# Handing out the closings of the cross-attention layer at a higher pace, and moving the rows' additions

## The chip, the cores and the metric

The kernel runs on one core of a Trainium2 chip. The metric is the device time of one execution in microseconds, as the median of several runs. The core has engines with in-order queues of their own: PE (TensorE, the matrix unit; PEld is its loading of weights), DVE (VectorE), ACT (ScalarE), POOL (GpSimd) and SP (SyncE, which here only issues transfers). An instruction waits on semaphores for what it needs, and everything behind it on its engine waits with it.

## The reference, cut to what matters

The model is four layers of cross-attention over 16 batches of 56 tokens (width 256), with a context of 1500 rows of width 128 per batch.

```python
x = _L0_xattn_ref(x, ctx, ...)         # memory attention and a gate
x = _L1_xattn_ref(x, ctx, mask, ...)   # 16 heads, context masked; then layernorm and a GELU feed-forward
x = _L2_xattn_ref(x, ctx, types, ...)  # third layer, below
x = _L3_xattn_ref(x, ctx, mask, ...)   # as L1 with other weights: the fourth layer

def _L2_xattn_ref(...):
    vm = expert_mask(token_type_ids)[..., None]
    mixed = jnp.where(vm, rms_norm(x) @ v_qkv, rms_norm(x) @ l_qkv)   # self-attention, rotary, causal
    x = x + jnp.where(vm, ctx @ v_dense, ctx @ l_dense)
    x = x + softmax(cq @ ck.T) @ cv @ cdense_w                        # 16 heads of 8 over 1500 rows
    mi = rms_norm(x, ln_post_attn_w)
    v_out = jax.nn.silu(mi @ v_gate) * (mi @ v_up) @ v_down
    l_out = jax.nn.silu(mi @ l_gate) * (mi @ l_up) @ l_down
    return x + jnp.where(vm, v_out, l_out)                            # the third layer's closing
```

## The kernel before, in words

Tokens go in four groups (0 to 3) of four batches each. Work items are (layer, group), 16 in all, item k = 4 * layer + group; the third layer is items 8 to 11, the fourth items 12 to 15. Each item has an opening (norm, projections), an attention, and a closing (output projection or feed-forward). While the attention of an item is emitted, a Python generator, the side work, gives out the closing of earlier items and the opening of the next one in pieces between the attention's own instructions. All of this only sets the order in which instructions are emitted and so their place in each engine's queue; on the chip the queues run as the semaphores let them.

**Third layer** (`att2`). Each batch b has six steps, j = 0 to 5. I number them 6 * b + j, from 0 to 95. `weights_pair` is the head of a step: four ones-times-shift products and sixteen key products into four PSUM banks (L1441, L1450), four exponentials on ACT (L1455), and additions of the weights into `all` (L1467), on POOL for all batches but the last, four per step (two in a step with j = 0). Beside it a step has `largest` (scores of batch b + 1 and after: L1404 into four banks, four maxima on DVE, L1409), `sums_chunk` (weights times values of the step before, L1482), and one of `values` (L1387) and `keys` (L1375). Step j = 4 makes the next batch's shift (`shifts`: L1417 to L1420 on DVE, L1424 on PE, the copy L1430 on DVE). Step j = 0 closes the previous batch's sums: a copy on ACT, a product with a mask on POOL (L1493), and a reduction on DVE (L1496). Step j = 1 has `own_sums` (L1508 on PE, which needs the batch's finished `all`; L1514, L1516 on DVE). From step 88 on no `largest` is left.

Two calls of `pace` in a step give out side work: the first after the step's head with the rate from `SHARES[group][behind]` (L1354), the second at its end. Each piece yields its cost in microseconds; a bare `yield` ends the call. If the first call made anything, `largest` is emitted ahead of `sums_chunk`, otherwise after it.

The third layer's closing, `post2`, runs for two groups at a time on rows sorted by token type: three rounds (one expert's rows, rows of both, the other's), each with transposes (L310), six gate and up products (L1642) and four pieces of down products (L1661). Its result goes to `made_rows` in DRAM. `fetch` gathers a group's rows back with two indirect transfers that POOL issues (L1679), and `take` adds them to x on DVE (L1689) and begins the fourth layer's norm: statistics on DVE (L339 to L344), a power on POOL (L320), and the normalised rows xn on POOL (L354). PE then transposes xn (L310), and the query projection follows (L907). `late()` holds the closing of groups 0 and 1 (between items 10 and 12), `fetch(0)`, `take(0)`, `fetch(1)`, `take(1)`, and the closing of groups 2 and 3, which goes into the fourth layer. `take`'s addition is tied to follow the instruction whose name is in `line["drained"]`: in the third layer the last maximum that `largest` emitted.

**Fourth layer** (`rows`). A batch is a unit, u00 to u15: seven score products S (L624), each with a masked minimum on DVE (L627) and an exponential on ACT (L631), and in the middle, after the third S, the weighted sum of the batch two units back, 48 products as built (L642, below AV), whose results DVE and ACT copy out (`rows_out`, L1020, L302). `rows_close` (L979) ends a pair of batches. Side work is stepped after each S. `beside(13)` holds `fetch(2)`, `fetch(3)`, `take(2)`, `take(3)`, then the opening of group 2; the closing of group 0 (`follows`: output projection L1092, norm, L1120, GELU L1127, L1092) came after that opening.

PSUM tiles of matmul results come from one ring of seven banks (`ps_s`): a new tile takes the bank of the seventh tile before it, and waits until that one has been read. The weights tile `pw` comes from a ring of three.

Of the kernel before, what the change touches and what calls it, by code (L numbers as in the profile page):

```python
# [62 lines left out]
def tile_kernel(ctx: ExitStack, tc: tile.TileContext, a, layers=4, groups=NG):  # L63
# [3 lines left out]
    nc = tc.nc  # L67
# [24 lines left out]
    def turn():  # L92
        return psum(ps_s, "sc")
# [4 lines left out]
    def few(w):  # L98
        return small.tile([128, w], F32, tag="few", bufs=8, name="few", padded_shape=[128, 16])
# [222 lines left out]
    def behind(made, name, reason):  # L322

        if name:
            tc.add_manual_dep(
                made.ins, name,
                mybir.DependencyInfo(
                    mybir.DependencyClass.NoSync, mybir.DependencyReason.DATA
                ),
                reason=reason,  # L330
            )
# [196 lines left out]
    def pace(share, kept, most):  # L528

        line["due"] += share  # L530
        made = False
        for _ in range(most):
            if line["due"] <= kept:
                break
            work = next(line["side"], line)
            if work is line:
                line["due"] = 0.0
            elif work:
                line["due"] -= work
                made = True  # L540
            else:
                line["due"] = min(line["due"], 3.0)
                break
        return made

    line, memory_w, halves_of, queries, heads_w, cross, held, begun = {}, [], {}, {}, {}, {}, {}, {}
# [804 lines left out]

    QH = 4 * N
    PAIRS = NC // 2
    SHARES = (2.1, 1.65), (2.1, 1.1), (2.1, 1.7), (1.9, 1.9)  # L1354

    def spread_queries(b):

# [55 lines left out]
    def shifts(b):  # L1413

        made = cross[b]
        nm = few(8)[: 2 * N]
        nc.vector.tensor_reduce(nm, made["mx"], AX.X, ALU.max, negate=True)  # L1417
        both = minus[b % 2]
        nc.vector.tensor_copy(both[:, :, 0].bitcast(F32R), nm)
        nc.vector.tensor_tensor(both[:, :, 1], nm, both[:, :, 0], ALU.subtract)  # L1420
        t = turn()
        for n in range(8):
            half, g = divmod(n, 4)
            nc.tensor.matmul(  # L1424
                t[g * BW : (g + 1) * BW, half * 2 * N : (half + 1) * 2 * N],
                both[:, n, :], ident[: 2 * N, : 2 * N], start=True, stop=True,
                skip_group_check=True,
            )
        shift = small.tile([128, QH], F32R, tag="shift", bufs=2, name="shift")
        nc.vector.tensor_copy(shift, t[:, :QH])  # L1430
        made["shift"] = shift

    def weights_pair(b, j):
# [119 lines left out]
    def att2(gi, state, then, ends):  # L1553

        for k in range(G):
            b = gi * G + k
            for j in range(PAIRS):
# [6 lines left out]
                weights_pair(b, j)  # L1564
                full = pace(SHARES[gi][line["behind"]], -0.8, 1)
                last, n = (b, 2 * j - 2) if j else (b - 1, NC - 2)
# [120 lines left out]
    def take(gi, y):  # L1687
        xf = xs[gi].rearrange("p i d -> p (i d)")
        behind(nc.vector.tensor_add(xf, xf, y), line["drained"], "banks go first")  # L1689
        if gi < 3:  # L1690
            begin_layernorm("L3_ln_q_g", gi)

    def program():
# [15 lines left out]
        def before(k):  # L1709
            if k + 1 < len(items):  # L1710
                states[k + 1] = yield from items[k + 1][0](items[k + 1][4])
# [7 lines left out]
        def beside(k):  # L1719

            yield from line.pop("rest", ())
            if k == len(items) and short:
                while line["closed"] < k:
                    yield
                yield from ending(k - 1, 1)
                return
            if k and k + 1 in (groups, groups + 1):
                begin_layernorm("L1_ln_q_g", k + 1 - groups)
            ahead = before(k)
            if k + 1 < groups:  # L1730
                yield next(ahead)
            if k == groups + 1:
                for rows, zeros in zip(sorted_rows, minus):
                    nc.sync.dma_start(
                        rows.rearrange("(p r) d -> p r d", p=TP),
                        zeros.rearrange("p n m -> p (n m)").unsqueeze(1).to_broadcast([TP, 6, D]),
                    )
            third = 2 * groups - 1 <= k <= 3 * groups
            if k:
                _, _, _, post, gi = items[k - 1]  # L1740
                follows = line["late"] if third else post(gi, states.get(k - 1))
            if k + 1 == 3 * groups:
                while line["stage"] < 3:
                    yield next(follows)
            if k == 3 * groups:
                yield next(follows)
            if k == 3 * groups + 1:
                while line["stage"] < 5:
                    yield next(line["late"], 0)
                yield  # L1750
                yield
                back = fetch(2), fetch(3)
                for _ in range(7):
                    yield
                take(2, back[0])
                yield
                take(3, back[1])
                yield
            if k > groups:
                for work in ahead:  # L1760
                    if isinstance(work, tuple):
                        line["beside"] = 1
                        while line["closed"] < k:
                            yield
                        for _ in range(work[1]):
                            yield next(follows, 0)
                    else:
                        yield work
            line["behind"] = 1
            if third:  # L1770
                if k + 1 == 2 * groups:
                    begin_norm("L2_ln_in_w", 1)
                while not line["end"] or line["stage"] < (0, 1, 2, 2, 4, 4)[k + 1 - 2 * groups]:
                    yield next(follows, 0)
                return
            if k:
                while line["closed"] < k:
                    yield
                yield from follows
                states.pop(k - 1)  # L1780
                if k > len(items) - groups:
                    nc.sync.dma_start(
                        a["out"][gi * T : (gi + 1) * T, :].rearrange("(i p) d -> p i d", p=TP), xs[gi]
                    )
            if k <= groups:
                yield from ahead
            if groups <= k < len(items) - 2:
                layer, group = divmod(k + 2, groups)
                if layer == 2:
                    begin_norm("L2_ln_in_w", group)  # L1790
                else:
                    begin_layernorm(f"L{layer}_ln_q_g", group)
            if k + 1 == len(items) and short:
                while line["pair"] != ("L3", groups - 1, 0):
                    yield
                yield from ending(k, 0)

        def late():

            third = 2 * groups  # L1800

            def at(k):
                return line["k"] > k or line["k"] == k and (line["behind"] or line["beside"])

            for gi in (groups - 2, groups - 1):
                while line["closed"] < groups + gi + 1:
                    yield
                yield from post13(
                    "L1", gi, states[groups + gi],
                    pause=lambda: not at(third if gi == groups - 2 else third + 1),  # L1810
                )
                begin_norm("L2_ln_in_w", gi)
                line["stage"] += 1
            while line["closed"] < third + 2 or not at(third + 2):
                yield
            yield from post2(0)
            yield
            yield
            y = fetch(0)
            for _ in range(4):  # L1820
                yield
            take(0, y)
            line["stage"] += 1
            y = fetch(1)
            for _ in range(4):
                yield
            take(1, y)
            line["stage"] += 1
            while line["closed"] < 3 * groups:
                yield  # L1830
            yield from post2(1)
            line["stage"] += 1

        def ending(k, i):

            _, _, _, post, gi = items[k]
            yield from post(gi, states[k], range(i, i + 1))
            at = gi * T + i * TP
            nc.sync.dma_start(a["out"][at : at + TP, :], xs[gi][:, i])
# [34 lines left out]
    t = turn()  # L1874
# [164 lines left out]
```

## Time and profile before

| | us |
|---|---|
| median of 3 runs (1436.54, 1442.94, 1444.49) | 1442.94 |
| the profiled execution's own time | 1437.15 |
| its span in the trace | 1435.3 |
| PE busy | 1357.3 (95%) |
| third layer: step 0 starts / step 82 / step 85 / step 88 / step 92 | 450.1 / 997.5 / 1016.7 / 1028.8 / 1056.2 |
| fourth layer: first S / u06 starts / u07 starts | 1069.5 / 1187.7 / 1214.7 |
| PE idle from 900 to 1070 / from 1070 to the end | 9.0 / 15.1 |

Starts of steps and units are read from the trace's instructions in order of time: a step starts with its first L1441, a unit with its first L624. In the listings below a timeline line reads: start, length (of merged instructions together), engine, line, operation, output<-input, count, and in brackets the idle time of the engine before it and what ended it. A line of the windows view reads: stretch, its length, then busy time of PE, PEld, DVE, ACT and POOL with counts, the granted PE clock (1.00 is full), DMA share and GB/s.

### The profile page before, as it was taken

The numbers are of one execution on the slowest core, as the hardware profiler recorded it, in microseconds if no ns is written. First come the engines' busy times: TensorE is split into PE (matmuls) and PEld (weight loads), VectorE is DVE, ScalarE is ACT, GpSimd is POOL, SyncE is SP. The second block draws the span as 40 slices with busy tenths as digits, with TensorE's granted clock in tenths as the row PEclk, the third lists the DMA queues.
The fourth block names the chain that finished last, engine by engine and source line by source line (L and its number), as shares of the span: only waits on it lengthen the run. The fifth ranks groups of instructions, "written<-read, shape, count | busy, mean of one in ns | idle before, by whom it ended". The sixth has DMA issues, their size and how long they took to land.

```text
span 1435.3 us, 32417 instructions
## 1 busy us (share of the span) xinstructions
PE 1357.3 (95%) x13638; PEld 938.2 (65%) x13638; DVE 777.7 (54%) x1794; ACT 744.8 (52%) x1703; POOL 526.2 (37%) x567
## 2 busy tenths in 40 slices
PE   6989999999899999999999999999899998999998
PEld 4667677775656556655555556656467776877776
DVE  4444754647575754467545755455565445455641
ACT  2334866756543547445554544444356565557661
POOL 0011001010101677767767768788743112100000
PEclk9999999999999999999999999999999999999998
DMA  7853224232322021110201022131122343333320
GB/s 270 351 191 126 85 89 145 90 112 65 103 76 81 23 82 52 54 56 24 81 31 43 29 71 68 52 103 56 39 82 94 134 152 101 124 118 123 108 89 10
DMA packets 38808, 135.78 MB, mean 95 GB/s; under 512 B 8605, under 2 KB 18493, under 8 KB 34557
## 3 DMA queue, kind: packets, MB, share of 16 engines
q1 hardware_dynamic: 33901, 119.03, 24.1%
q0 software_dynamic: 2592, 10.85, 2.2%
q10 hardware_dynamic: 2160, 3.74, 0.8%
q8 instruction: 109, 1.79, 0.5%
q14 instruction: 46, 0.38, 0.1%
HBM read 129.01 MB, written 4.59 MB: 93 GB/s over the span
## 4 chain that ended last, share of the span: by engine, by line
PE 75%; DVE 12%; ACT 6%; POOL 3%; DMA 3%; issue 1%; SPq 0%; DVEq 0%; POOLq 0%; ACTq 0%
PE sc L642 9%; PE sc L624 8%; PE sc L1092 7%; PE sc L1404 7%; PE sc L1450 4%; PE o L1482 4%; PE sc L1642 4%; DVE mx L1409 3%; PE sc L907 3%; PE sc L1120 3%; PE sc L1387 3%; PE sc L1441 3%; PE sc L1661 2%; PE sc L1375 2%; POOL all L1467 2%; ACT p L302 2%
## 5 line engine op out<-in xcount | busy, mean ns | idle before, releaser
L1467 POOL TENSOR_TENSOR all<-all,pw 125x448 f32<-125x448 f32 x300 | 341.1, 1149 | 125.8 <-ACT pw L1455 114.7
L1409 DVE TENSOR_REDUCE mx<-sc 112x1 f32<-112x500 f32 x384 | 233.4, 669 | 140.6 <-PE sc L1404 140.5
L1455 ACT ACTIVATE pw<-sc 125x448 f32<-125x448 f32 x384 | 177.7, 550 | 102.8 <-PE sc L1450 100.1
L631 ACT ACTIVATE p<-p,few 128x384 f32<-128x384 f32 x224 | 136.9, 611 | 99.3 <-DVE few L627 98.9
L624 PE MATMUL sc<-ktl,qa 128*128 128x384 f32 x448 | 176.9, 504 | 0.0
L627 DVE CUSTOM_DVE_ANT_0 p<-sc,mkl 128x384 f32<-128x384 f32 x224 | 121.8, 551 | 92.1 <-PE sc L624 87.4
L642 PE MATMUL sc<-p,kvl 32*128 32x224 f32 x2160 | 149.5, 353 | 4.7 <-DVE qa L940 3.3
L642 PEld LDWEIGHTS sc<-p,kvl 32*128 32x128 f32 x2160 | 136.3, 185 | 20.5 <-issue 9.6
L642 PE MATMUL o<-p,kvl 32*128 32x224 f32 x720 | 144.6, 352 | 0.0
L143 POOL TENSOR_SCALAR mkl<-m32l 128x384 bf16<-128x384 uint8 x32 | 16.3, 510 | 314.1 <-DVE few L627 292.5
L642 PEld LDWEIGHTS o<-p,kvl 32*128 32x128 f32 x720 | 130.7, 185 | 0.0
L302 ACT ACTIVATE p<-p,few 128x384 f32<-128x384 f32 x224 | 121.1, 608 | 8.6 <-DVE few L618 7.2
L1404 PE MATMUL sc<-ck,qs 32*112 32x500 f32 x768 | 122.5, 626 | 2.8 <-ACT ck L302 1.4
L661 DVE STREAM_TRANSPOSE p<-p 128x768 f32<-128x768 f32 (+1 forms) x96 | 102.8, 1095 | 28.6 <-ACT p L302 28.4
L624 PEld LDWEIGHTS sc<-ktl,qa 128*128 128x128 f32 x448 | 78.8, 190 | 37.4 <-issue 9.0
L1450 PE MATMUL sc<-qs,ck 32*125 32x224 f32 x1536 | 98.8, 355 | 0.0
L320 POOL TENSOR_TENSOR stat<-stat,half_less 112x2 f32<-112x2 f32 (+1 forms) x33 | 23.1, 700 | 201.8 <-DVE stat L344 162.0
L302 ACT ACTIVATE ot<-sc 128x224 f32<-128x224 f32 x64 | 32.0, 609 | 121.1 <-PE o L642 83.5
L1482 PE MATMUL o<-pw,vc 125*32 125x224 f32 x1536 | 93.0, 359 | 0.0
L1482 PEld LDWEIGHTS o<-pw,vc 125*32 125x32 f32 x1536 | 40.2, 109 | 69.9 <-issue 57.2
L1450 PEld LDWEIGHTS sc<-qs,ck 32*125 32x125 f32 x1536 | 77.4, 183 | 1.1
L302 ACT ACTIVATE vc<-sc 125x512 f32<-125x512 f32 x48 | 28.6, 596 | 82.0 <-PE sc L1387 79.2
(286 smaller groups left out, 2360.7 us busy)
## 6 DMA issues: line engine op xcount, KB each, us to landing
kvl<-in_ctx_last SPq DMA_DIRECT2D x30, 768.0 KB, 4.2
kt<-in_ctxT SPq DMA_DIRECT2D x23, 750.0 KB, 5.0
w<-in_L_W SPq DMA_DIRECT2D x16, 1024.0 KB, 4.8
w<-in_L_Wq SPq DMA_DIRECT2D x8, 1024.0 KB, 5.0
w<-in_L_Wo SPq DMA_DIRECT2D x8, 1024.0 KB, 5.6
ktl<-in_ctxT SPq DMA_DIRECT2D x32, 192.0 KB, 2.5
w<-in_L_v_qkv SPq DMA_DIRECT2D x4, 768.0 KB, 6.8
w<-in_L_l_qkv SPq DMA_DIRECT2D x4, 768.0 KB, 4.1
```

Source lines behind the costliest of these rows:

```text
L302: nc.scalar.activation(out, in_, AF.Copy, scale=scale)
L624: line["scored"] = nc.tensor.matmul(sc[:, :LW], u["q"][:, i * 128 : (i + 1) * 128], u["kt"], start=True, stop=True).ins.name
L627: line["drained"] = nc.vector.tensor_tensor_reduce(u["p"][:, i], sc[:, :LW], u["mask"], 1.0, -LOWEST, ALU.add, ALU.min, mn[:, i : i + 1],) ...
L631: nc.scalar.activation(u["p"][:, i], u["p"][:, i], AF.Exp, bias=mn[:, i : i + 1], scale=-1.0, accum_out=den[:, i : i + 1],)
L642: product = nc.tensor.matmul(o[g][:, : RB * BW], y["kv"][part, j, :], y["p"][part, :, j * BW : (j + 1) * BW], start=j == 0, stop=j == LB - ...
L661: nc.vector.transpose(blocks, blocks)
L1404: nc.tensor.matmul(banks[g][: 2 * N, :SW], made["q"][part, rows], made["k"][part, cols], start=True, stop=True,)
L1409: line["drained"] = nc.vector.tensor_reduce(made["mx"][:, half * 4 + g, s : s + 1], banks[g][: 2 * N, :SW], AX.X, ALU.max).ins.name
L1450: nc.tensor.matmul(banks[g][:CP, c * QH : (c + 1) * QH], made["k"][part, at : at + CP], made["q"][part], start=False, stop=c == 1, skip_gr ...
L1455: line["weighed"] = nc.scalar.activation(p[:, :, g * QH : (g + 1) * QH], banks[g][:CP, : 2 * QH].rearrange("p (c n) -> p c n", c=2), AF.Ex ...
L1467: added = engine.tensor_tensor(made["all"][:, cols], made["all"][:, cols] if j else p[:, 0, cols], p[:, c, cols], ALU.add,)
L1482: nc.tensor.matmul(made["o"][part, :QH], made["v"][:, n, part], p[:, r * QH : (r + 1) * QH], start=n == 0, stop=n + 1 == NC, skip_group_ch ...
```

## The change

In the third layer the pace of groups 2 and 3 goes up (1.7 to 2.0 and 1.9 to 2.15). `shifts` now puts its copy's name into `line["drained"]`, so that an addition in `take` stands behind a shift copy if that was emitted last. `late()` gives five bare yields instead of four between `fetch(0)` and `take(0)`. In the fourth layer, `beside(13)` waits until item 12 has closed, and gives out five pieces of the closing of group 0 between fetch and addition, and one more after each addition.

```diff
-    SHARES = (2.1, 1.65), (2.1, 1.1), (2.1, 1.7), (1.9, 1.9)
+    SHARES = (2.1, 1.65), (2.1, 1.1), (2.1, 2.0), (2.15, 2.15)
@@ shifts
-        nc.vector.tensor_copy(shift, t[:, :QH])
+        line["drained"] = nc.vector.tensor_copy(shift, t[:, :QH]).ins.name
@@ beside
             if k == 3 * groups + 1:
                 while line["stage"] < 5:
                     yield next(line["late"], 0)
-                yield
-                yield
+                for _ in range(4):
+                    yield
                 back = fetch(2), fetch(3)
-                for _ in range(7):
+                while line["closed"] < k:
                     yield
+                for _ in range(5):
+                    yield next(follows, 0)
                 take(2, back[0])
-                yield
+                yield next(follows, 0)
                 take(3, back[1])
-                yield
+                yield next(follows, 0)
@@ late, after fetch(0)
-            for _ in range(4):
+            for _ in range(5):
                 yield
```

What this does to the built order of instructions in the program that runs: up to step 64 the two builds are equal. Pieces of closing and opening that stand in each of the last steps (PE order; "before/after largest" tells whether L1482 stands behind or ahead of L1404):

| step | before | after |
|---|---|---|
| 65, 66 | one L1661 piece each | two L1661 pieces each |
| 82 | L1661 piece, before | none, after |
| 83 | two L1661 pieces, before | none, after |
| 84 (batch 14, j = 0) | L1661 piece, before | none, after |
| 85 | none | none |
| 86 | none | L310 of xn of group 0, then two L907 pieces |
| 87 | none | two L907 pieces |
| 88 | L310 of xn of group 0 | none |
| 89 | three L907 pieces | none |
| 90 | one L907 piece | none |

On POOL, `fetch(0)` stood after step 86's additions and now stands between step 83's and step 84's; `fetch(1)` stood after step 88's and now stands after step 85's, directly ahead of the power and xn of group 0; xn of group 1 stood among step 89's additions and now stands ahead of them. On DVE, `take(0)` stood between step 87's maxima and the shift of batch 15 and now stands behind step 85's maxima; `take(1)` now stands behind batch 15's shift copy. In step 84, L1496 now stands ahead of that step's four maxima; before, it stood behind them.

In the fourth layer, with S, AV, T (L310), Q (L907), dn (L1092) and up (L1120), counts in instructions as built, units 6 and 7 read on PE:

```
before  u06: S S S AV48 S S S T1 S T3 Q16 qa16
        u07: S dn8 S dn8 S AV48 S T4 S up1 S up7 up4 wv16 up4 dn16
after   u06: S dn4 S dn8 S dn4 AV48 S S T4 S T1 S T3 Q16 up4 qa16
        u07: S up8 S up4 dn4 S dn2 AV2 dn2 AV46 S dn4 S dn4 S S wv16
```

All other units are equal. ACT gets two more loads of a function table in units 6 and 7 (36 instead of 34 in the program that runs). On SP the loads of the closing's weights (Wo, W1, W2 of group 0) now stand ahead of Wq of group 2.

## The prediction

> **What bounds the kernel now.** I read the page first: PE is busy 95% of the span, so only PE's idle time and its clock can move the total; the change moves products but adds none. Then the two stretches that it touches: PE's timeline with its idle times, POOL's beside it, then DVE's, and last the windows view for the clock.
>
> The page's costliest groups: four L1467 additions a step are 4.6 us of POOL, four maxima 2.4 us of DVE.
>
> ```profile
> L1467 POOL TENSOR_TENSOR all<-all,pw 125x448 f32<-125x448 f32 x300 | 341.1, 1149 | 125.8 <-ACT pw L1455 114.7
> L1409 DVE TENSOR_REDUCE mx<-sc 112x1 f32<-112x500 f32 x384 | 233.4, 669 | 140.6 <-PE sc L1404 140.5
> ```
>
> PE at the end of the third layer: in steps 60 to 87 it idles 0.1 us, then 6.3 us in step 88, for the shift (late behind `take(0)` on DVE) and for xn.
>
> ```profile
> 1030.15 0.47 PE L1441 MATMUL sc<-shift,ones_r 2*125 2x448 f32 x1 [0.42 <-DVE mx L1409]
> 1035.20 0.97 PE L1424 MATMUL sc<-ident,minus 112*32 112x112 f32 x16 [2.93 <-DVE minus L1420]
> 1038.37 0.45 PE L310 MATMUL sc<-ident,xn 112*128 112x112 f32 x1 [2.19 <-POOL xn L354]
> 1039.58 0.82 PE L310 MATMUL sc<-ident,xn 112*128 112x112 f32 x3 [0.76 <-POOL xn L354]
> ```
>
> POOL there, almost without a break; xn stands behind step 87's additions:
>
> ```profile
> 1019.11 4.66 POOL L1467 TENSOR_TENSOR all<-all,pw 125x448 f32<-125x448 f32 x4 [2.35 <-ACT pw L1455]
> 1023.93 4.65 POOL L1467 TENSOR_TENSOR all<-all,pw 125x448 f32<-125x448 f32 x4 [0.16 <-ACT pw L1455]
> 1028.73 1.01 POOL L1679 DMA_INDIRECT back<-made,place  x1
> ...
> 1036.25 0.73 POOL L320 TENSOR_TENSOR stat<-stat,half_less 112x2 f32<-112x2 f32 x1
> 1037.09 2.43 POOL L354 TENSOR_SCALAR xn<-x,stat 112x256 f32<-112x256 f32 x2
> ```
>
> DVE in step 48, where L1496 stands ahead of the maxima as it will in step 84: it waits for POOL, and the maxima start 2.8 us after their products.
>
> ```profile
> 775.85 0.54 DVE L1496 TENSOR_REDUCE rest<-rest 128x56 f32<-128x224 f32 x1 [3.04 <-POOL rest L1493]
> 776.31 2.42 DVE L1409 TENSOR_REDUCE mx<-sc 112x1 f32<-112x500 f32 x4
> ```
>
> The fourth layer's one large wait, in u06:
>
> ```profile
> 1196.11 0.68 DVE L1689 TENSOR_TENSOR x<-x,back 112x512 f32<-112x512 f32 x1
> 1199.23 0.16 DVE L344 TENSOR_SCALAR stat<-stat 112x2 f32<-112x2 f32 x1
> 1201.61 0.34 PE L310 MATMUL sc<-ident,xn 112*128 112x112 f32 x1 [4.86 <-POOL xn L354]
> ```
>
> After both waits the granted clock is halved:
>
> ```profile
> 1034.60:1044.70 10.10, 6.55 (x46) 4.76 (x47) 2.89 (x9) 1.85 (x4) 9.47 (x10) 0.50 0.01 2
> 1201.80:1208.50 6.70, 6.10 (x17) 4.63 (x17) 2.97 (x6) 2.34 (x5) 1.48 (x2) 0.50 0.22 39
> ```
>
> At half the clock the busy time holds half the work: 3.3 and 3.05 us lost.
>
> **The third layer.** Pieces given out sooner (steps 65 to 81) cost nothing: PE has no idle time there to fill or add, and a longer step gives POOL and DVE more room. The result's copy and write leave ACT a step's work before step 82, 12 us ahead of the gather, and wait for nobody.
>
> From step 82 I set t = 0 at its start. Before, steps 82 to 84 took 6.00 + 7.35 + 5.82 = 19.2 us with four L1661 pieces; the same without them are steps 46, 47 and 86: 5.03 + 4.52 + 4.54 = 14.1. So the pieces are worth 5.1 us, and t = 0 is at 997.5 + 5.1 = 1002.6.
>
> A step's first exponential comes 1.3 us after its head, its additions 2.4 us after (1016.67 to 1019.11). Additions of 82: 2.4 to 7.05; of 83 (head at 5.0): 7.4 to 12.1. Then `fetch(0)`, 2.3 us (1028.73 to 1031.01): 14.5. Then step 84's two additions (2.2) and L1493 (0.56): 17.3. Only now can L1496 run, and behind it step 84's maxima. Step 85's head, due at 14.1, needs in the ring of seven the banks of two of step 84's score tiles for its third and fourth tile: 17.3 + 0.5 + two maxima of 0.6 = 19.0. **Wait A**, 4.5 us; no piece covers it, as the L1241 pieces did in step 48.
>
> Step 85's exponentials then start at 20.2, its additions end at 25.9, `fetch(1)` at 28.3. `take(0)` runs behind step 85's maxima at 24.7 (rows long landed); addition 1.15, statistics and its neighbours L1514 and L1516 about 3: 28.8. Power 0.75, xn 2.43: the first half at 30.8, the second at 32.0. PE reaches the transposes at 25.3. **Wait B**: 5.5 + 0.8 = 6.3 us, where step 88's 6.3 and 0.2 in step 91 go away. The shift of 15 is late no more: L1417 to L1420 are done before L1424 in step 88.
>
> Step 87 starts at 39, 88 at 46 (heads 1.4; L1482 0.9; L1404 1.0; L1387 1.1; four L907 pieces of 1.65). Step 88's additions end at 52.9; power and xn of group 1, now ahead of step 89's additions, at 56; those at 60.7. L1508 of step 91 needs them and PE is there at 55.8, since steps 89 and 90 have lost their L907 pieces. **Wait C**: 4.9 us. POOL is the engine that is late next all through.
>
> Clock: after A and B 6.8 us each at half, about 6 busy, as after 1201.8. A's loss delays POOL's input too and is taken partly out of B (net 1.8), B's counts (3.0), C's falls where DVE sets the pace (0.5); before 3.3. Net +2.0. After C, L1496 of batch 14 does not stand behind xn: -0.9 (1055.56 to 1056.75 before).
>
> Sum: 4.5 + 6.3 + 4.9 - 6.5 + 2.0 - 0.9 = **+10.3 us**. Bounds: A at least 0 (banks free in time, as in step 86) and at most 4.5 with the whole 3.05 of its clock; C at least 0 with no clock loss (POOL level with PE, as in steps 60 to 81) and at most 6.5, with additions at the 5.13 us that four took beside DVE at 1031.01. So 10.3 - 6.3 - 5.4 = -1.4 to 10.3 + 1.2 + 1.6 = +13.1; I take the chain's value, as each of its links is a row of the same stage.
>
> **The fourth layer.** dn16 moves from u07 to u06, ahead of AV; its weights are issued where Wq and Wo were (1166.7, 1167.4), 20 us early. Wq waits for Wo's buffer until dn16 ends, AV covers it (Q16 is over 12 us later, the page's 1 MB of Wq lands in 5.0). It is passed on SP by no load that PE needs in u06. On POOL the four issues stay in place. But `take(2)` still stands behind AV's copies on DVE: AV's end to xn was 1194.6 to 1201.6, 7.0 us, and stays so. PE has three S (2.05 us) and now T4 (0.5) in it: the wait goes from 4.86 to 4.4, its clock loss stays. Against it, dn now follows up more closely, with table loads between: 0.78 and 1.16 us in front of L1092 in u11 and u15; AV2 covers most. The two table loads (1.283 us by their row) run on ACT, 15.6 of 27 us busy in u06: nothing. Sum 0; bounds -7.9 (wait and clock loss gone) and +2 (both L1092 waits).
>
> In "ScalarE: Activation LUTs" of the Trainium skill, "What ACT_TABLE_LOAD costs", a switch is a load of about 1283 ns and a drain of about 1380. The row of before has no drain: load at 1233.14, GELU at 1234.44. By the page ACT would lose 5.3 us instead of 2.6, and PE still nothing. "TensorE: Matmul & The Clock Gate", "Why this matters for your kernels", warns of idle gaps over about 3 us; here the clock fell after 2.93 and 2.19 us with work between. By the page waits A and B would each halve the clock, which speaks against the change as the rows do; without any such loss the sum would be 2.0 us less.
>
> **Rivals.**
> - *Only waits B and C* (step 84's DVE order does not hold up PE, for instance since POOL runs ahead): A and its net clock loss go, 10.3 - 6.3 = +4: 1447. Against it: the 3.04 us row of step 48.
> - *Landing was the brake* (ends faster): additions waited for their rows (DVE's timeline has 0.91 and 6.91 us of waiting for back, at 1032.76 and 1048.28). With more steps between, xn would be ready at both transposes: 6.3 + 3.3 and 4.86 + 3.05 us go, 1425. It decides from 7.2 us on, so if xn comes within 2 us of PE at both places. Against it: the rows had landed in u06 too, and POOL and AV set the time there.
> - *No change beyond the order* (A and C both stay away, B takes the place of the old 6.3 us with its clock): 10.3 - 6.3 - 5.4 = -1.4, 1442. For it: POOL kept up in every step before 85.
> - *Slower still*: the third layer's upper bound and both L1092 waits, 13.1 + 2 = +15: 1458.
>
> **How the numbers follow.** The profiled execution took 1437.15, 5.8 us below the median of 1442.94; +10.3 + 0 on the median gives 1453 (1447 to 1457 for this case alone). Chances: forecast 0.58, slower still 0.12, only B and C 0.12, no change 0.10, landing 0.08. 0.5% is 7.2 us, about what a measurement of this kernel tells from no change. Slower: 0.70; same: 0.22; faster: 0.08. The range, without 0.08 below and 0.07 above, is 1440 to 1460.
>
> **What would show it.** After: L1496 of step 84 waiting some 4 us on POOL and step 85's third L1441 on DVE; L310 in step 86 waiting over 4 us on POOL; L1508 of step 91 on POOL; two or three stretches at 0.50; in u06 still 4 us before L310. Wrong if step 85's head comes at once, or if u06's L310 does not wait.

## The result, and the profile after

| | before | after |
|---|---|---|
| median of 9 runs each, us | 1440.61 (1434.03 to 1444.49) | 1450.06 (1443.85 to 1455.03) |
| ratio, with its 95% interval | | 1.0071 (1.0050 to 1.0092) |
| profiled execution, own time / span | 1437.15 / 1435.3 | 1449.21 / 1447.4 |
| step 60 to step 82 | 141.2 | 147.6 |
| step 82 to the fourth layer's first S | 72.0 | 77.3 |
| the two together | 213.3 | 224.9 |
| u06 and u07 | 59.1 | 58.6 |
| first S of u08 to first S of u15 / from there to the end | 119.5 / 69.0 | 119.8 / 69.3 |

The change makes the kernel slower by 0.7%, some 10 us. The forecast was 1453 on a median of 1442.94, a ratio of 1.007. The third layer lost 11.6 us; in the fourth, u06 and u07 won half a microsecond, and the units behind them lost 0.6. All of this is read from step 60 on: the profiled execution of after reaches that step 0.57 us later than that of before, which is no part of the change.

One caution for every stage that is compared with before: its profiled execution was a lucky one. Its own time, 1437.15 us, is 3.5 us below the median of 1440.61, and its mean granted clock was 0.986; of the 75 executions of before that ran beside the experiments, two had 0.986 or more, and their mean was 0.982. After's profiled execution is 0.9 us below its median. So the profile flatters before, by 3.5 to 5.2 us against its medians here.

The page of the kernel after first: span, busy time, and the granted clock in 40 slices.

```profile
span 1447.4 us, 32415 instructions
PE 1364.0 (94%) x13638; PEld 940.5 (65%) x13638; DVE 775.6 (54%) x1794; ACT 749.1 (52%) x1705; POOL 525.5 (36%) x567
...
PEclk9999999999999999999999999999889999999998
```

PE is busy 6.7 us longer for the same 13638 products (1357.3 before), and the clock row has two slices of 8 where the third layer ends: time lost at half clock counts as busy. The idle part is on PE's timeline. Between 1010 and 1075 us these are the five longest pauses, with the wait in brackets:

```profile
1022.73 1.31 PE L1441 MATMUL sc<-shift,ones_r 2*125 2x448 f32 x2 [4.08 <-DVE mx L1409]
1036.04 0.36 PE L310 MATMUL sc<-ident,xn 112*128 112x112 f32 x1 [3.76 <-POOL xn L354]
1037.25 0.82 PE L310 MATMUL sc<-ident,xn 112*128 112x112 f32 x3 [0.85 <-POOL xn L354]
1066.21 0.40 PE L1508 MATMUL sc<-all,l2w 125*32 125x56 f32 x4 [4.37 <-POOL all L1467]
1068.51 0.96 PE L1508 MATMUL sc<-all,l2w 125*32 125x56 f32 x28 [1.89 <-POOL all L1467]
```

They are waits A (step 85), B (step 86, in two halves of xn) and C (step 91, in two halves of `all`), at the places forecast. The old 6.3 us of step 88 are gone. DVE's timeline shows A's cause: the reduction L1496 holds up the four maxima behind it while it waits for POOL's L1493.

```profile
1021.55 0.53 DVE L1496 TENSOR_REDUCE rest<-rest 128x56 f32<-128x224 f32 x1 [6.41 <-POOL rest L1493]
1022.00 2.42 DVE L1409 TENSOR_REDUCE mx<-sc 112x1 f32<-112x500 f32 x4
```

POOL's timeline, from `fetch(0)` to xn of group 0:

```profile
1016.51 1.01 POOL L1679 DMA_INDIRECT back<-made,place  x1 [0.16 <-issue]
1017.83 0.94 POOL L1679 DMA_INDIRECT back<-made,place  x1 [0.30 <-issue]
1018.79 2.22 POOL L1467 TENSOR_TENSOR all<-pw 125x448 f32<-125x448 f32 x2
1020.96 0.56 POOL L1493 TENSOR_TENSOR rest<-rest,tables 128x224 f32<-128x224 f32 x1
1026.41 4.64 POOL L1467 TENSOR_TENSOR all<-all,pw 125x448 f32<-125x448 f32 x4 [4.88 <-ACT pw L1455]
1031.19 0.96 POOL L1679 DMA_INDIRECT back<-made,place  x1
...
1034.76 2.43 POOL L354 TENSOR_SCALAR xn<-x,stat 112x256 f32<-112x256 f32 x2
```

Read it downwards: the two issues of the fetch delay step 84's additions and L1493; PE then waits (A) and brings no new weights, so POOL itself is idle for 4.88 us, until step 85's exponentials; then step 85's additions and `fetch(1)` stand ahead of xn (B). Since POOL idles in the middle of its own backlog, its total (525.5 us) says nothing of the loss.

The windows view in the stretches behind the waits; the granted clock is the third value from the right.

```profile
1022.50:1029.40 6.90, 6.67 (x58) 3.19 (x62) 2.17 (x5) 1.86 (x4) 2.92 (x3) 0.51 0.00 0
1036.20:1043.00 6.80, 5.95 (x34) 2.93 (x34) 2.23 (x5) 0.00 (x0) 5.44 (x5) 0.50 0.01 2
1063.50:1073.70 10.20, 5.59 (x72) 3.52 (x74) 4.16 (x9) 1.86 (x4) 5.32 (x6) 0.50 0.00 0
1220.50:1227.30 6.80, 6.15 (x18) 4.62 (x17) 3.25 (x9) 2.56 (x6) 4.53 (x5) 0.50 0.15 36
```

Behind A and B 6.83 us at half clock each, behind C 10.24, and in u06 the 6.83 that were there before. That wait in u06 is still on the timeline: the addition stands behind AV's copies on DVE, and the normalised rows xn and their transposes follow from it.

```profile
1215.00 0.69 DVE L1689 TENSOR_TENSOR x<-x,back 112x512 f32<-112x512 f32 x1
...
1218.93 2.44 POOL L354 TENSOR_SCALAR xn<-x,stat 112x256 f32<-112x256 f32 x2
...
1220.22 0.32 PE L310 MATMUL sc<-ident,xn 112*128 112x112 f32 x1 [4.05 <-POOL xn L354]
```

### The profile page after: what moved, and what is told of

It reads as the page before. It is cut to its first block, busy times and chain, and to the rows that moved or that the text cites. A ratio compares the mean times of both kernels' runs of the same rounds, so it can differ in the third digit from the quotient of the medians.

```text
span 1447.4 us, 32415 instructions
## 1 busy us (share of the span) xinstructions
PE 1364.0 (94%) x13638; PEld 940.5 (65%) x13638; DVE 775.6 (54%) x1794; ACT 749.1 (52%) x1705; POOL 525.5 (36%) x567
## 5 line engine op out<-in xcount | busy, mean ns | idle before, releaser
L1404 PE MATMUL sc<-ck,qs 32*112 32x500 f32 x768 | 124.2, 631 | 2.8 <-ACT ck L302 1.4
L1482 PE MATMUL o<-pw,vc 125*32 125x224 f32 x1536 | 95.1, 366 | 0.2 <-ACT rest L302 0.2
L1482 PEld LDWEIGHTS o<-pw,vc 125*32 125x32 f32 x1536 | 40.8, 110 | 69.7 <-issue 56.8
```

What stands on the lines that cost most here:

```text
L1404: nc.tensor.matmul(banks[g][: 2 * N, :SW], made["q"][part, rows], made["k"][part, cols], start=True, stop=True,)
L1482: nc.tensor.matmul(made["o"][part, :QH], made["v"][:, n, part], p[:, r * QH : (r + 1) * QH], start=n == 0, stop=n + 1 == NC, skip_group_ch ...
```

## The experiments

Twelve kernels were run, each against the kernel before. "Third" is the stretch from step 60 to the fourth layer's first S in the profiled execution, in us; its part from step 82 on is called the tail (72.0 us in before, 77.3 in after). The stage carries a doubt of its own: run e2 has the third layer of before unchanged and measured 216.2 instead of 213.3, from one stretch at half clock that is told of at the end.

| run | kernel | ratio to before | 95% interval | third | u06+u07 |
|---|---|---|---|---|---|
| | before | 1 | | 213.3 | 59.1 |
| | after | 1.0071 | 1.0050 to 1.0092 | 224.9 | 58.6 |
| e1 | before + pace | 1.0007 | 0.9988 to 1.0026 | 219.2 | 59.4 |
| e2 | before + fourth layer's part | 0.9994 | 0.9973 to 1.0015 | 216.2 | 58.7 |
| e3 | after, maxima first | 1.0010 | 0.9990 to 1.0030 | 220.1 | 58.6 |
| e4 | after, three pieces | 1.0028 | 0.9999 to 1.0057 | 224.2 | 53.9 |
| e5 | after, four bare yields | 1.0013 | 0.9999 to 1.0027 | 217.3 | 58.4 |
| e6 | after, additions on DVE | 1.0082 | 1.0061 to 1.0103 | 222.4 | 59.5 |
| e7 | before + tie and fifth yield | 1.0001 | 0.9988 to 1.0014 | 216.4 | 59.0 |
| e8 | after, e3 + e4 + e5 + e6 | 0.9949 | 0.9931 to 0.9966 | 214.0 | 53.2 |
| e9 | after, e3 + e4 + e5 | 0.9972 | 0.9953 to 0.9991 | 216.0 | 55.6 |
| e10 | e8, two moves at the end | 0.9932 | 0.9907 to 0.9958 | 211.0 | 55.8 |
| e11 | e10, transposes one call later | 0.9905 | 0.9875 to 0.9934 | 207.5 | 55.7 |
| e12 | before + fourth layer's part with three pieces | 0.9950 | 0.9931 to 0.9970 | 213.3 | 55.7 |

**e1: the pace alone.** On the kernel before:

```diff
-    SHARES = (2.1, 1.65), (2.1, 1.1), (2.1, 1.7), (1.9, 1.9)
+    SHARES = (2.1, 1.65), (2.1, 1.1), (2.1, 2.0), (2.15, 2.15)
```

> The kernel before with the two higher rates of the third layer alone. Theory (order on POOL and DVE sets the loss, and the pace alone brings it): L1496 of step 84 again stands ahead of that step's maxima, so PE waits some 4 us at step 85's third L1441 with a half clock behind it; the transposes of group 0's xn, now in step 85, wait 3 to 6 us for POOL; L1508 of step 91 waits 4 to 7 us for POOL. The whole third layer is 8 to 14 us longer than before, the time 1.006 to 1.010 of before. Rival (the loss comes from tying the additions to the shift copies and from the fifth bare yield): within 3 us of before, none of the three waits over 2 us.

A miss. The two waits of the theory are there, 4.07 us in step 85 and 4.20 + 1.89 us in step 91, but B is not: PE does not wait for xn at all (the shift of batch 15 is late by 1.63 us instead). The third layer is 5.9 us longer rather than 8 to 14, and that in an execution that was the slowest of its ten (1448.40 us, their median 1444.32); the time is within 0.3% of before. So the pace alone is not the loss, although it brings A and C; the rival that put it down to tie and fifth yield alone is wrong too, since A and C came with the pace.

**e2: the fourth layer's part alone**, the second hunk of the change on the kernel before.

> The kernel before with the change of the fourth layer alone. Theory: no change that can be measured, -0.5 us within 2 either way: L310 in u06 still waits about 4 us for POOL's xn, since the addition stays behind AV's copies on DVE, and the half clock after it stays. Rival (the steps between fetch and addition are worth something): the wait and its half clock go, 6 to 8 us faster than before, 0.995. Third possibility: dn and GELU closer together cost PE waits at L1092, 2 us slower.

As the theory had it: no change (u06 and u07 together 0.4 us shorter). The addition still stands behind AV's copies.

**e3: step 84's maxima first.** On the kernel after, so that L1496 comes behind the maxima:

```diff
-                full = pace(SHARES[gi][line["behind"]], -0.8, 1)
+                full = pace(SHARES[gi][line["behind"]], -0.8, 1) or (b == B - 2 and not j)
```

> The changed kernel with step 84's maxima (and their products) emitted ahead of its sums, so that L1496 stands behind them on DVE. Theory of the chain on POOL: wait A of 4.1 us in step 85 and the half clock there go away, but POOL's chain (additions of 85, fetch, power, xn) only moves up by some 4.4 us, to the end of step 84's additions, so the wait in step 86 grows from 4.6 to about 8 us, L310 starts near 1031.6 instead of 1036.0, and the whole is 4 to 5 us shorter than the changed kernel: 1.004 of before. Rival 1 (each wait is worth its length and its half clock): 8 us shorter than the changed kernel, 1.0015 of before, the wait in step 86 stays at 4.6. Rival 2 (the banks are not held up by the maxima but by something else): step 85 stays at 12.6 us.

Step 85 now takes 4.70 us instead of 12.59, with no idle time. PE's timeline of this kernel where B was:

```profile
1034.59 0.45 PE L310 MATMUL sc<-ident,xn 112*128 112x112 f32 x1 [5.80 <-POOL xn L354]
1035.80 0.82 PE L310 MATMUL sc<-ident,xn 112*128 112x112 f32 x3 [0.76 <-POOL xn L354]
```

B has grown from 4.61 to 6.56 us, less than the 8 expected. Counted from the start of step 82, L310 starts at 26.5 us instead of 31.6; the third layer is 4.8 us shorter, not 8. Of A's 7.9 us (wait and half clock) 4.8 are saved; step 86, with B and its half clock, is 2.5 us longer, and step 84 0.5. In the trace the theory of one POOL chain holds, with 5.1 us instead of its 4.4. The time does not say so: 1.0010 is below the expected 1.004, which lies outside its interval, and nearer to the 1.0015 of rival 1. From after's 1.0071 that would be some 9 us, but with both intervals 5 to 13, so the 4.8 us are at its edge.

**e4: three pieces instead of five in the fourth layer**, on the kernel after.

```diff
-                for _ in range(5):
+                for _ in range(3):
                     yield next(follows, 0)
                 take(2, back[0])
```

> The changed kernel with three instead of five pieces of the closing given out between fetch and additions in the fourth layer: the two additions come to stand ahead of AV's copies on DVE, and xn is made while AV runs. Theory (the place on DVE behind AV sets u06's wait): L310's wait of 4.05 us and most of the 6.83 us at half clock after it go, u06 and u07 together 6 to 7.5 us shorter than in the changed kernel (58.6): 1.002 of before. Rival (the rows land late or POOL is late): the wait stays at 2 us or more and the clock still falls, 0 to 3 us shorter.

u06 and u07 take 53.9 us instead of 58.6, the wait before L310 is gone and so is the half clock in u06. The saving is 4.7, not 6 to 7.5, because the next thing to be late is the other closing's norm: in u07 PE now waits 2.92 us at L1120. The time, 1.0028, is near the expected 1.002; its interval still touches after's.

**e5: four bare yields**, on the kernel after.

```diff
-            for _ in range(5):
+            for _ in range(4):
                 yield
             take(0, y)
```

> The changed kernel with four bare yields between fetch(0) and take(0), as before the change; pace, tied shift copy and fourth layer stay changed. Theory (the fifth yield puts take(0) one call later, and so xn of group 0 behind step 85's additions and fetch(1) on POOL): xn is made in POOL's idle time before step 85's additions, wait B of 4.6 us in step 86 shrinks to under 1.5 us with its half clock, and from step 82 to the fourth layer's first product it takes 71 to 73 us, as with the pace alone, instead of 77.3: 1.0025 of before. Rival (the tie to the shift copy, or the pace, makes wait B): 76 to 78 us stay, 1.007.

In the traces this is the largest single piece; in the time e3 (1.0010) and e5 (1.0013) do not differ. POOL's timeline of this kernel:

```profile
1024.09 0.56 POOL L1493 TENSOR_TENSOR rest<-rest,tables 128x224 f32<-128x224 f32 x1
1029.44 0.73 POOL L320 TENSOR_TENSOR stat<-stat,half_less 112x2 f32<-112x2 f32 x1 [4.79 <-DVE stat L344]
1030.29 2.44 POOL L354 TENSOR_SCALAR xn<-x,stat 112x256 f32<-112x256 f32 x2
1032.70 4.64 POOL L1467 TENSOR_TENSOR all<-all,pw 125x448 f32<-125x448 f32 x4
```

With one yield less `take(0)` follows step 84's maxima. Power and xn fall into the time in which POOL waits anyway because of A, ahead of step 85's additions, and B is gone. The tail is 69.7 us instead of 77.3, and the time goes from 1.0071 to 1.0013. The expectation (71 to 73; 1.0025) was too cautious.

**e6: batch 14's last eight additions on DVE**, on the kernel after.

```diff
-                engine = nc.gpsimd if b + 1 < B else nc.vector
+                engine = nc.gpsimd if (b, j) < (B - 2, 4) else nc.vector
...
-                if b + 1 < B:
+                if engine is nc.gpsimd:
                     line["added"] = added.ins.name
```

> The changed kernel with the additions of batch 14 in steps 88 and 89 on DVE (0.62 us each there for batch 15) instead of POOL (1.15 us each). Theory (wait C is POOL's additions, late since nothing of the side work is left for PE in steps 88 to 91): L1508 of step 91 waits under 1.5 us instead of 6.3, the 10.24 us at half clock behind it go, the whole is 6 to 8 us shorter than the changed kernel: 1.002 of before. Rival (DVE is as full: the eight additions, 5 us, push batch 15's additions and take(1) back, and PE waits in steps 92 to 95 instead): 0 to 3 us shorter.

Wait C is gone, and nothing is won: the rival was right. PE's timeline of this kernel:

```profile
1061.89 0.59 PE L1508 MATMUL sc<-all,l2w 125*32 125x56 f32 x28 [0.41 <-DVE all L1467]
1067.21 1.15 PE L929 MATMUL sc<-qT,wl 64*128 64x112 f32 x16 [1.60 <-DVE rest L1514]
1070.50 0.73 PE L1441 MATMUL sc<-shift,ones_r 2*125 2x448 f32 x1 [1.74 <-DVE qa L940]
```

In after, C had covered what comes next on DVE: L1514 behind the L1496 that waits for POOL, and the copies L940 behind four of batch 15's additions. With C gone, PE runs into both, and the clock falls there instead (6.83 us at half). The third layer is 2.5 us shorter in the profile; the ratio, 1.0082 from four executions, does not differ from after's beyond the two intervals.

**e7: the tie and the fifth yield without the pace**, on the kernel before.

```diff
-        nc.vector.tensor_copy(shift, t[:, :QH])
+        line["drained"] = nc.vector.tensor_copy(shift, t[:, :QH]).ins.name
...
-            for _ in range(4):
+            for _ in range(5):
                 yield
             take(0, y)
```

> The kernel before with the tied shift copy and the fifth bare yield alone, without pace and fourth layer. Theory (place on POOL decides): batch 15's shift is late no more, but take(0) comes behind it, xn of group 0 stands behind the additions of steps 87 and 88 and fetch(1) on POOL, and PE reaches its transposes in step 89 some 2 us after step 88's head: the wait there is 9 to 12 us instead of 6.3, the whole 3 to 7 us longer than before, 1.002 to 1.005. Rival (the tie does what its place suggests: shift early, nothing else late): the 6.3 us and the half clock behind them go, 6 to 9 us shorter, 0.995.

Most of the mechanism came as expected; PE's timeline of this kernel, in step 89:

```profile
1047.55 0.45 PE L310 MATMUL sc<-ident,xn 112*128 112x112 f32 x1 [9.96 <-POOL xn L354]
1049.21 0.82 PE L310 MATMUL sc<-ident,xn 112*128 112x112 f32 x3 [1.22 <-POOL xn L354]
```

11.2 us of waiting for xn, which stands behind eight additions (9.69 us) and `fetch(1)`. The shift is still late in step 88, by 1.18 us, so that steps 88 and 89 wait 12.8 us in all where before had 6.3; the two later waits of before (0.74 and 1.74 us, below) shrink to 0.69. The profiled third layer is 3.1 us longer. The time, however, is unchanged (1.0001), and the expected 1.002 to 1.005 lies outside of its interval. That part of the expectation failed. The clocks of the single executions tell why the profiles mislead: the two profiled executions differ by 5.5 us with granted clocks of 0.986 and 0.983, but the ten executions of e7 and the 22 of before beside them both have 0.983 in the mean. Where a usual execution of before loses what its profiled one did not is not shown; the 2.9 us in e2's third layer are one such place.

**e8: four parts at once**: e3, e4, e5 and e6 on the kernel after.

> The changed kernel with four parts at once: four bare yields, step 84's maxima ahead, batch 14's last eight additions on DVE, and three pieces instead of five in the fourth layer. Theory (the waits A, B, C and u06's are separate costs, each with its half clock, where A and B lie on one chain of POOL): A 0, B under 2 us, C under 1.5, u06 under 1; 14 to 18 us shorter than the changed kernel and 4 to 8 us shorter than before: 0.995 to 0.997. Rival (POOL's sum of work in steps 84 to 91 sets the end, so that one wait grows as another goes): the third layer's tail from step 82 stays at 70 us or more, 1.000.

0.9949, the first kernel that is faster than before, as the theory said. A is gone, C is gone, u06 has no wait before L310. B is 2.08 + 0.90 us, not under 2, and it is no longer POOL's queue that sets it: the addition in front of the norm now waits for its rows to land, and POOL waits for the addition. DVE's row and POOL's of this kernel:

```profile
1017.45 1.05 DVE L1689 TENSOR_TENSOR x<-x,back 112x512 f32<-112x512 f32 x1 [2.16 <-DMA back<-made,place]
1020.38 0.73 POOL L320 TENSOR_TENSOR stat<-stat,half_less 112x2 f32<-112x2 f32 x1 [1.47 <-DVE stat L344]
```

The tail is 66.5 us against 77.3 in after. Two waits of 1.60 and 1.74 us in steps 92 and 93 stay, with 10.24 us at half clock behind them.

**e9: the same without the additions on DVE.**

> The kernel of the last run (four bare yields, maxima first, three pieces in the fourth layer), but with batch 14's additions all on POOL again. Theory (POOL's wait C and the waits of steps 92 and 93 for DVE take each other's place, so that the eight additions on DVE were worth little): L1508 of step 91 waits 5 to 6.5 us, the waits of 1.60 and 1.74 us in steps 92 and 93 are gone, from step 82 to the fourth layer's first product 66 to 69 us instead of 66.5, 0.995 to 0.998 of before. Rival (wait C is a cost of its own): 71 to 73 us, 0.999 to 1.001.

C is back (4.05 + 1.89 us), the waits in steps 92 and 93 are gone but for 0.33 us, and the tail is 68.4 us: C and those two waits take each other's place, as e6 had suggested. The eight additions are worth 1.9 us in the tail; the intervals of e8 and e9 overlap.

**e10: two more moves**, on e8, for those two waits.

```diff
-                engine = nc.gpsimd if (b, j) < (B - 2, 4) else nc.vector
+                engine = nc.gpsimd if (b, j) < (B - 2, 4) or (b, j) == (B - 1, 2) else nc.vector
...
-            nc.gpsimd.tensor_tensor(
+            (nc.vector if b == B - 2 else nc.gpsimd).tensor_tensor(
                 raw, raw, m_own.unsqueeze(2).to_broadcast([128, 4, N]), ALU.mult
```

> The same with the eight additions on DVE and two more moves: L1493 of batch 14 on DVE instead of POOL, and step 92's four additions of batch 15 on POOL instead of DVE. Theory (L1496 waits for L1493 behind xn on POOL, and the copies L940 stand behind additions on DVE; both hold up PE in steps 92 and 93, and the 10.24 us at half clock follow from these two waits): both waits under 0.6 us, the half clock there gone, from step 82 to the fourth layer 59 to 62 us instead of 66.5, 0.990 to 0.992 of before. Rival (PE is ahead of ACT's exponentials or of DVE there anyway, and waits at another place): 64 to 67 us, 0.994.

Half a hit. Both waits shrink (1.60 to 0.36, 1.74 to 0.88 us), and the tail is 63.4 us, short of the 59 to 62. The half clock did not go with the waits: 6.83 us of it still begin at 1060 us. The ratio, 0.9932, lies between theory and rival.

**e11: the transposes of xn one call later**, on e10.

```diff
                 while line["stage"] < 3:
                     yield next(follows)
+                yield next(follows, 0)
```

> The same as the tail run, with the transposes of group 0's xn and its query products given out one call later (the transposes behind step 86's head). Theory (the rest of wait B, 2.09 and 0.90 us in step 85, only needs a step's work on PE in front): the wait falls under 0.5 us and its 3.41 us at half clock go, 3 to 5 us shorter than the tail run: 0.987 to 0.989 of before. Rival (POOL's sum sets the end, the wait moves to the next place): within 1.5 us of the tail run.

The waits over 0.4 us that are left in the tail, on PE's timeline:

```profile
1047.29 0.47 PE L1441 MATMUL sc<-shift,ones_r 2*125 2x448 f32 x4 [0.52 <-DVE shift L1430]
1052.25 0.59 PE L1508 MATMUL sc<-all,l2w 125*32 125x56 f32 x28 [0.42 <-DVE all L1467]
1058.78 0.73 PE L1441 MATMUL sc<-shift,ones_r 2*125 2x448 f32 x1 [0.89 <-DVE qa L940]
```

The transposes stand in step 86, where they stood in after, and wait for nothing, since xn was made ahead of step 85's additions; the addition waits 2.16 us for its rows here too, but the transposes come late enough. The tail is 59.9 us, 3.5 less than in e10, as the theory had it, and 17.4 less than in after. The median of four executions is 1428.49 us against 1442.22 of before beside it, 0.9905 (0.9875 to 0.9934), a little above the expected 0.987 to 0.989: this version beats both kernels.

**e12: the fourth layer's part with three pieces, on the kernel before.**

> The kernel before with the change of the fourth layer alone, but three pieces instead of five. Theory (the place of the additions ahead of AV on DVE is worth u06's wait and its half clock, and is independent of the third layer): u06's L310 waits under 1 us, u06 and u07 together 53 to 55 us instead of 59.1, 4 to 6 us faster than before, 0.996. Rival (only together with the third layer's order): 1.000.

0.9950: the edit that e4 showed on after works on before as well. u06 and u07 take 55.7 us, not quite the 53 to 55: 3.41 us at half clock follow the new wait in u07, which e4 did not have. That the medians differ by 6.6 us and not by 3.4 is the caution of the first section again. PE's timeline of this kernel has no wait before the transposes, and the new one in u07:

```profile
1204.57 0.55 PE L310 MATMUL sc<-ident,xn 112*128 112x112 f32 x4
1206.68 0.65 PE L907 MATMUL sc<-xT,w 128*128 128x224 f32 x2 [0.90 <-DVE xT L379]
...
1220.41 0.65 PE L1120 MATMUL sc<-xT,w 128*128 128x224 f32 x2 [2.92 <-DVE xT L379]
```

With five pieces (e2) the same edit was worth nothing. The two additions have to stand ahead of AV on DVE; the number of pieces alone decides that.

## Why the prediction was right

The direction, the size and the three waits were right. That the sum comes so close is in part luck: A and B together came 2.1 us smaller than forecast, C and its half clock 3.5 larger. By the forecast's own terms, in us:

| term | forecast | after |
|---|---|---|
| start of step 85 against before (pieces worth 5.1) | 0 | +0.9 |
| wait A | 4.5 | 4.08 |
| wait B | 6.3 | 4.61 |
| half clock of A and B (A's net 1.8, B's 3.0) | 4.8 | 5.5 |
| wait C, with the 0.2 in front of L1482 | 4.9 | 6.46 |
| half clock of C, and the end | 0.5 - 0.9 | 2.4 - 2.5 |
| taken away: step 88's wait, 0.2 in step 91, clock | -9.8 | -9.3 |
| other products of steps 87 to 93 | 0 | -0.5 |
| sum | +10.3 | +11.7 |

How the right column is read: A, B, C are the waits shown above. The half clock of A and B is busy time of steps 85 and 86 (8.51 + 10.99 us) less that of the same steps in e11, where the clock was full (4.69 + 9.35): 5.5. For C it is step 91's and 92's busy time against e11's (3.50 + 6.01 less 2.80 + 4.30): 2.4. Before's two DVE waits in steps 92 and 93 (0.74 and 1.74) are what the end gives back. Step 85 starts at 1018.2 - 0.6 = 1017.6 against 1016.7: the products L1404 take 0.9 us more in steps 60 to 84. In "taken away" the clock is 2.8 us instead of 3.3: before's busy time of steps 85 to 92 is 37.2 us, that of e11, with the same products at full clock, 34.5. The sum is the third layer's 11.6 us but for rounding; by the medians the loss is 9.5 us.

- **The start.** "The pieces are worth 5.1": the stretch from step 60 to step 82 grew by 6.4, and steps 82 to 84 lost 5.4 instead of 5.1.
- **Wait A** came for the reason given. e3 took it away by the order on DVE alone. Its price by itself was mis-sized: the rival "only waits B and C" put it at 6.3 us with its net clock, and e3 measured 4.8 in the third layer, since POOL's chain holds the end.
- **Wait B** was the term that was furthest off among the waits, 6.3 for 4.61, because the half clock behind A delays PE by 3.8 us and POOL's xn by less than one. The forecast had that as A's net clock. What it did not say is that the fifth bare yield is what puts xn there: e5, with four, has no B, and its tail is 7.6 us shorter; e1, with the pace alone, has none either. The forecast read xn's place from the finished order and so had the effect without the cause. With B and its clock out of its sum, 10.3 - 6.3 - 3.0 = +1.0 us would be left; e1 measured 1.0007 and e5 1.0013, +1.0 and +1.9 us.
- **Wait C** was too small. Counted from step 88's start, POOL ended step 89's additions after 15.6 us instead of 14.7 (step 88's additions took 5.00 us for 4.65, the power 1.09 for 0.73), and PE was at L1508 after 9.0 instead of 9.8. Its clock was sized wrongly: instead of 0.5 us, 2.4 were lost, as the clock was low for 10.24 us.
- **The fourth layer at 0** was right (58.6 for 59.1, 4.05 for the 4.4 forecast), and so was its reason: e2 and e12 differ in two pieces, and so in whether the additions stand ahead of AV. The two table loads cost PE nothing, since in u06 and u07 PE has no wait over 0.3 us but the one for xn and 0.65 us behind it.
- **The rivals.** That the landing was the brake is excluded by after itself: none of its four additions (at 1031.51, 1055.80, 1215.00 and 1216.83 us) waits for its rows, and it is slower; in the fourth layer also by e12, where rows, fetch and issues are those of e2 and xn is in time. Only with A and B removed does it show, in e8 to e10. The forecast's hint that a wait removed brings out the next was the part that mattered most for the experiments: e3, e4 and e6 each ran into it.

Of the Trainium skill, "TensorE: Matmul & The Clock Gate", "Why this matters for your kernels", warns of idle gaps above some 3 us. A and C, at 4.08 and 4.37 us, agree. The 10.24 us behind 1.60 and 1.74 us in e8 do not: PE was between two waits there, not idle for 3 us.

## What to carry to other kernels

When one engine serves two purposes in order (here POOL: additions for the attention now, and the norm of the next layer), work that is handed out sooner must be followed through that engine's queue: one yield more put 2.4 us of xn behind 7 us of additions and fetch, and made the tail 7.6 us longer. A wait that is taken away shows what it had covered, so the value of an edit is measured with its neighbours: the additions on DVE were worth nothing alone and some 0.2% beside three others (e8 against e9, with intervals that overlap). And before work is spread between a fetch and its use, look at which instruction stands ahead of the use on its own engine; there, two pieces more or fewer decided 0.4% (e2 against e12). Last, edits that cost nothing one by one can cost together: pace (1.0007), tie and yield (1.0001) and the fourth layer's part (0.9994) were each level with before, all three together 1.0071.

## What the runs showed of the hardware that was not expected

The granted clock falls after shorter waits than those that the forecast went by, and not each time. In the same third layer, two waits in steps 92 and 93 left the clock full in before and halved it in e2. PE's timeline of before, then of e2:

```profile
1060.10 1.15 PE L929 MATMUL sc<-qT,wl 64*128 64x112 f32 x16 [0.74 <-DVE rest L1514]
1063.38 0.47 PE L1441 MATMUL sc<-shift,ones_r 2*125 2x448 f32 x1 [1.74 <-DVE qa L940]
```

```profile
1057.98 1.15 PE L929 MATMUL sc<-qT,wl 64*128 64x112 f32 x16 [0.75 <-DVE rest L1514]
1061.27 0.73 PE L1441 MATMUL sc<-shift,ones_r 2*125 2x448 f32 x1 [1.75 <-DVE qa L940]
```

The windows view of before, and then of e2, over the steps behind these waits:

```profile
1063.00:1069.40 6.40, 6.01 (x105) 3.85 (x105) 5.07 (x12) 4.30 (x10) 0.00 (x0) 1.00 0.01 3
```

```profile
1060.90:1067.30 6.40, 6.03 (x57) 3.67 (x61) 3.62 (x9) 1.85 (x4) 0.00 (x0) 0.50 0.01 3
```

The same length holds 105 products in the one and 57 in the other. In e10 even waits of 0.36 and 0.88 us, among steps of small products, had 6.83 us at half clock behind them:

```profile
1060.10:1066.50 6.40, 6.40 (x65) 3.30 (x57) 2.91 (x6) 3.08 (x7) 1.22 (x2) 0.50 0.01 3
```

The stretches at half clock were 3.41, 6.83 or 10.24 us long, in e7 one of 13.65: multiples of 3.41, but for the last one of a trace, which its end cuts off. They also start on a grid. In before they start at 31.00, 44.65, 379.15, 822.89, 1034.51 and 1201.77 us, which is 4.0, 98.0, 130.0, 62.0 and 49.0 times 3.413 us apart, and each of the other traces has such a grid, at a place of its own. "TensorE: Matmul & The Clock Gate", "What's actually happening", gives a window of that length that runs free of the kernel, 3413 ns; the grids agree.

Cut into these windows, the fourteen traces from step 60 to the end of u08 have 1587 windows that begin at full clock, and after 42 of them the clock was halved. A window in which PE, by its timeline, idled 2.0 us or more was always followed by half clock (31 windows), one with less than 1.2 us never; from 1.2 to 2.0 us the clock fell after 11 windows and stayed full after 15. So it is the idle time within one window that goes with the fall, rather than the length of one wait: around the two waits e2 idled 1.87 us in a single window, before 0.91 and 1.56 us in two. What decides between 1.2 and 2.0 us is not shown.

The same additions of 125x448 take 1.15 us on POOL and 0.62 on DVE, a factor of 1.9; "GPSIMD Engine Reference", "4.1 Engine selection", has about two for two inputs. One-input work the page calls roughly line-rate on POOL; L354, with one tile and its statistics as input, took 1.24 us a half on POOL and 0.41 on DVE, a factor of 3 (means of the kernel before). An indirect fetch of a group costs POOL 2.3 us in issues alone, two of 0.9 to 1.0 with 0.3 between; wait A was 4.08.
